# A two-layer hybrid block on one core: a scan step in another order, and Toeplitz tiles loaded in 32 rows and filled on the chip

## The chip, the cores and the metric

The kernel runs on one core of a Trainium2 chip. Its time is the time in microseconds (us) of one execution on the device; three runs of a kernel are given with their median. The profile is one more execution, recorded by the hardware profiler.

Five engines work side by side and wait for each other through semaphores: PE (TensorE, matmuls; its weight loads are listed apart as PEld), DVE (VectorE, elementwise work and reductions), ACT (ScalarE, activation functions and copies), POOL (GpSimd) and SP (SyncE, which only issues DMAs). Each engine takes its instructions strictly in the order of its own queue. An instruction that waits for a semaphore holds up everything behind it on that engine. SP, ACT and POOL can issue DMAs; an issue stands in the engine's queue like any other instruction.

## The reference, cut to what matters

The program is eight sublayers in a row, each added to x (2 x 2048 tokens of 256). Two of them are touched. The first is a selective scan: for each of 256 channels and 16 complex states a serial recurrence over 2048 tokens.

```python
def step(h, inp):
    x_t, dt_t, B_t, C_t, xr_t = inp
    h_carrier = h.mean(axis=1)
    T = jnp.cos((c_phase(xr_t) - c_phase(h_carrier)) / 2.0) ** 2
    alpha = jnp.exp(dt_t[..., None] * A_neg)
    expo = 1.0 + (1.0 - alpha) * KAPPA * (1.0 - T[:, None, :])
    mag, ph = (c_mag(h), c_phase(h))
    cmag = jnp.minimum(jnp.exp(expo * jnp.log(mag + 1e-08)), 10.0)
    h = from_polar(cmag, ph)
    Bx = B_t[:, None, :, :] * (dt_t * x_t)[:, :, None, None]
    h = h + Bx
    h = from_polar(jnp.tanh(c_mag(h)), c_phase(h))
    y_t = jnp.einsum('bnc,bdnc->bd', C_t, h)
    return (h, y_t)
```

The fifth is a long convolution: a projection to 512 channels, a four-tap convolution with SiLU, a convolution over 1024 taps with a filter of its own for each channel (written as an FFT, computed in the kernel as products with Toeplitz matrices), a gate and a projection back.

```python
x_f = jnp.fft.rfft(x, n=n)
k_f = jnp.fft.rfft(k_ssm, n=n)
y = jnp.fft.irfft(x_f * k_f[None], n=n)[..., :Lq]
y = y + x * D_skip[None, :, None]
y = y * _silu(z)
return jnp.einsum('bhl,dh->bld', y, W_out)
```

## The kernel before, in words

**Scan** (method scan, lines 257 to 550). The state is kept as real and imaginary part in tiles of 128 partitions x 64 elements. A hardware loop of four turns holds 32 groups of 16 steps each, all written out, under a manual schedule: every engine gets its instructions in the order in which the source names them. One step (lines 400 to 489) goes round like this:

- PE multiplies the channel sums hs with the constant mean into hc and hd (line 410), then projects the state of the step before to the output (line 494).
- ACT squares hc (line 418) and makes ci (427, 428). Meanwhile DVE works through gl (414), the product with hd (420), ex (424) and ngd (425). ACT makes ea from ex (429) and fac from ngd and ci (439).
- DVE forms the new state p (436 to 444) and its squared magnitudes m2 and r1 (446 to 453). ACT scales the drive of the next step meanwhile (391).
- ACT then runs twelve activations of 128x64 in a row (459 to 473): logarithms and exponentials that give 1/|h| (ir), e = exp(-2|h|), le = log(1+e), ld = log(1-e), sg = 1/(1+e), 1/|h|^2 (rm) and the small corrections k1 and k2c.
- DVE multiplies p by ir and by e-1 (475, 477), makes dl (480), multiplies by sg into the history tile with the sums hs as a second output (482), and ends with th, kc, lg and kd (486 to 489), which the next step's gl and ex read.

Several results live in small PSUM tiles of the pool pa with one buffer for each name: lm, m (used for le again) and lr (used for lb, the logarithm with 1e-8, again).

**Convolution** (method sublayer_c, lines 1073 to 1244). E = 4 blocks of 128 channels. For each block, kernels(e, g) loads Toeplitz tiles: partition p of a tile row holds the reversed filter from element p on, so one filter read at 64 shifted starts gives 64 rows. A group g is eight channels: SP loads partitions 0 to 63 with four of them, ACT partitions 64 to 127 with four others, 1216 elements long. The pool has three tiles. convolve then issues 9 x 2 x 4 x 2 matmuls of 64 rows x 32 columns with 128 moving columns (line 1170); the input xring is kept as two half blocks of 64 tokens by turn, which transposes with 16 matmuls a chunk (1154). After four groups leave copies the sums out of PSUM on ACT (1181) and stores them to DRAM from ACT's queue (1183). In even groups produce makes a chunk of the next block's input (PE line 1128, ACT copy 1134, DVE 1137 and 1139, ACT SiLU 1141, a POOL store) and finish takes up a chunk of the block before (POOL loads 1190 and 1191, PE 1195, ACT SiLU 1197, DVE 1198 and 1199). In odd groups turn and project follow (PE 1206, DVE 1210). In this part only PE's order is the order of the source; the order of the other engines is a scheduler's.

Of the kernel before, what the change touches and what calls it, by code (L numbers as in the profile page):

```python
# [17 lines left out]
AF = mybir.ActivationFunctionType  # L18
ALU = mybir.AluOpType
# [4 lines left out]
P = 128  # L24
B, S, D = 2, 2048, 256
NT = B * S
NI = NT // P
NB = S // P
# [9 lines left out]
SMALL = 1e-10  # L38
MAG_EPS = 1e-8
# [8 lines left out]
L_CONV = 1024  # L48
TOEP = L_CONV + P
KREV = 1280  # L50
# [3 lines left out]
HALF = P // 2  # L54
# [5 lines left out]
def new(pool, shape, name, **kw):  # L60
    return pool.tile(list(shape), F32, name=name, tag=name, **kw)


class Kernel:
# [192 lines left out]
    def scan(self, y, dtd, dxd, tabd):  # L257
# [6 lines left out]
        tc, nc = self.tc, self.nc  # L264
        V, A, G = nc.vector, nc.scalar, nc.gpsimd
        J, TURN = 64, TG * GROUPS
        with ExitStack() as c:
# [132 lines left out]
            def step(k, g, before, act_gap, dve_gap):  # L400
# [4 lines left out]
                hn = hist[g][:, k]  # L405
# [63 lines left out]
                A.activation(sg, le, AF.Exp, scale=-1.0)  # L469
# [3 lines left out]
                A.activation(k2c, lb, AF.Exp, scale=-0.5)  # L473
                for k2 in range(2):
                    V.tensor_tensor(p[:, k2], p[:, k2], ir, ALU.mult)  # L475
                for k2 in range(2):
                    V.scalar_tensor_tensor(p[:, k2], e, -1.0, p[:, k2], ALU.add, ALU.mult)  # L477
                th, kc, dl = (w([J], n) for n in ("th", "kc", "dl"))

                V.scalar_tensor_tensor(dl, p[:, 0], 0.5 * SMALL, rm, ALU.mult, ALU.mult)  # L480
                for k2 in range(2):
                    V.tensor_tensor_reduce(  # L482
                        out=hn[:, k2], in0=p[:, k2], in1=sg, scale=-1.0, scalar=0.0 if k2 else J * SMALL,
# [1 line left out]
                    )  # L485
                V.tensor_tensor(th, ld, le, ALU.subtract)
                V.scalar_tensor_tensor(kc, k2c, 2.0 * MAG_EPS, k1, ALU.mult, ALU.add)
                V.scalar_tensor_tensor(lg[o], th, 2.0, kc, ALU.mult, ALU.add)
                V.scalar_tensor_tensor(kd[o], kc, 0.5, dl, ALU.mult, ALU.add)

# [582 lines left out]
    def sublayer_c(self):  # L1073
# [7 lines left out]
        tc, nc = self.tc, self.nc  # L1081
        V, A, G = nc.vector, nc.scalar, nc.gpsimd
        E, TAPS = 4, L_CONV // P
        W = L_CONV + P + HALF
        with ExitStack() as c:
            dp = c.enter_context(tc.tile_pool(name="c_dram", bufs=1, space=DRAM))
            yd = dp.tile([E * P, NB, B, P], F32, name="c_yd", tag="c_yd")
# [8 lines left out]
            xring = [new(kp, [P, HALF, 2, TAPS + NB, B], f"c_x{j}") for j in range(2)]  # L1096
            for t in xring:
                G.memset(t[:, :, :, 0:TAPS], 0.0)
# [12 lines left out]

            with tc.tile_pool(name="c_ln", bufs=2) as lp, tc.tile_pool(name="c_pl", bufs=2, space=PSUM) as pl:
# [10 lines left out]
            def produce(e, ch):  # L1123

                b, i0, cs = ch // 4, ch % 4 * 4, slice(ch * CH, (ch + 1) * CH)
                ps = new(pp, [P, CH], "ps")
                for k in range(2):
                    nc.tensor.matmul(ps, wi[:, k, e * P : (e + 1) * P], xT[:, k, cs], start=k == 0, stop=k == 1)
                xin = new(xp, [P, 3 + CH], "c_xi")
                if i0 == 0:  # L1130
                    V.memset(xin[:, 0:3], 0.0)
                else:
                    V.tensor_copy(xin[:, 0:3], last[0][:, CH : CH + 3])
                A.copy(xin[:, 3:], ps)
                last[0] = xin
                acc = new(tp, [P, CH], "c_acc")
                V.tensor_scalar(acc, xin[:, 0:CH], cw[:, e, 0:1], cb[:, e : e + 1], ALU.mult, ALU.add)
                for j in range(1, 4):
                    V.scalar_tensor_tensor(acc, xin[:, j : j + CH], cw[:, e, j : j + 1], acc, ALU.mult, ALU.add)
                xs = new(tp, [P, CH], "c_xs")  # L1140
                A.activation(xs, acc, AF.Silu)
                G.dma_start(out=xd[e * P : (e + 1) * P, cs], in_=xs)
                return e, ch, xs

            def turn(e, ch, xs):

                b, i0 = ch // 4, ch % 4 * 4
                ps = new(pt, [P, 2, 4, HALF], "ps_t")
                for h in range(2):
                    for j in range(4):  # L1150
                        for r in range(2):
                            rows = slice(r * HALF, (r + 1) * HALF)
                            lo = j * P + h * HALF
                            nc.tensor.matmul(
                                ps[rows, h, j, :], xs[:, lo : lo + HALF], self.ident[:, rows], start=True, stop=True
                            )
                for h in range(2):
                    V.tensor_copy(
                        xring[e % 2][:, :, h, TAPS + i0 : TAPS + i0 + 4, b], ps[:, h].rearrange("p j c -> p c j")
                    )  # L1160

            def convolve(e, g, t, ps):
                x = xring[e % 2]
                for m in range(TAPS + 1):
                    for h in range(2):
                        lo = L_CONV - m * P + h * HALF
                        for j in range(4):
                            for r in range(2):
                                rows = slice(r * HALF, (r + 1) * HALF)
                                nc.tensor.matmul(  # L1170
                                    ps[r][j * 32 : (j + 1) * 32, g % 4, :],
                                    x[rows, 4 * g + j, h, TAPS - m : TAPS - m + NB, :].rearrange("p i b -> p (i b)"),
                                    t[rows, j, lo : lo + P],
                                    start=m == 0 and h == 0, stop=m == TAPS and h == 1,
                                )

            def leave(e, g, ps):

                for r in range(2):
                    ys = new(tp, [P, 4, P], "c_ys")  # L1180
                    A.copy(ys, ps[r][:, :, ::-1])
                    rows = slice(e * P + r * HALF + 4 * g, e * P + r * HALF + 4 * g + 16)
                    A.dma_start(
                        out=yd[rows].rearrange("(s j) i b t -> (j i b) s t", j=4), in_=ys
                    )

            def finish(e, ch):
                b, i0, cs = ch // 4, ch % 4 * 4, slice(ch * CH, (ch + 1) * CH)
                yc, xs = new(tp, [P, CH], "c_yc"), new(tp, [P, CH], "c_xs")
                G.dma_start(out=yc.rearrange("p (i t) -> p i t", t=P), in_=yd[e * P : (e + 1) * P, i0 : i0 + 4, b])  # L1190
                G.dma_start(out=xs, in_=xd[e * P : (e + 1) * P, cs])
                ps = new(pp, [P, CH], "ps")
                z0 = E * P + e * P
                for k in range(2):
                    nc.tensor.matmul(ps, wi[:, k, z0 : z0 + P], xT[:, k, cs], start=k == 0, stop=k == 1)
                sz = new(tp, [P, CH], "c_acc")
                A.activation(sz, ps, AF.Silu)
# [24 lines left out]
                later(turn, t)  # L1222
            later(turn)
            for e in range(E):
                for g in range(HALF // 4):
                    t = kernels(e, g)
                    if g % 4 == 0:
                        ps = [new(pc, [P, 4, P], f"ps_c{r}") for r in range(2)]
                    convolve(e, g, t, ps)
                    if g % 4 == 3:  # L1230
                        leave(e, g - 3, ps)
                    if g % 2 == 0:
                        work = []
                        if e + 1 < E:
                            work.append((turn, produce(e + 1, g // 2)))
                        if e > 0:
                            work.append((project, finish(e - 1, g // 2)))
# [469 lines left out]
```

## Time and profile before

| | us |
|---|---|
| median of three runs | 14147.37 (14145.97 to 14152.4) |
| profiled execution, its own time | 14151.41 |
| its span, first to last instruction | 14149.7 |
| up to the scan's loop | 335 |
| after the scan, up to the convolution's start (10170 to 11095) | 925 |
| norm and first chunks of the convolution (11095 to 11171) | 76 |
| after the convolution's loop (from 12170) | 1980 |

Over the span DVE is busy 10378.9 us, ACT 8647.8, PE 5571.1 and POOL 415.6. The longest waits inside the scan, from the view of who waited for whom (engine, line, released by: total us, times, longest):

```profile
ACT lm L459 <- DVE m L451: 1216.4, 2047, 1.1
ACT sq L418 <- PE hc L410: 1168.8, 2043, 0.9
DVE p L475 <- ACT ir L463: 1063.2, 2047, 0.6
...
DVE p L436 <- ACT ea L429: 323.1, 2047, 1.6
```

They are the places of a step at which one engine stands until another hands over: each occurs once in each of the 2048 steps. A wait on a line says nothing of what comes behind it in the same queue; for that the timeline is read. In the page and the timeline a tile is named by what the program called it, with numbers left out, so m stands for m, m2 and le, and lr for lr, ln and lb.

### The profile page before, as it was taken

What the parts mean: (1) busy time and instruction counts of PE and PEld (TensorE: products, weight loads), DVE (VectorE), ACT (ScalarE), POOL (GpSimd) and SP (SyncE); (2) the same over time, 40 slices, a digit from 0 to 9 for tenths busy, and PEclk for the clock granted to TensorE, in tenths of its full rate; (3) what the DMA queues carried; (4) which work ended last, traced back from release to release, by engine and by line L of the source; (5) the groups of instructions that cost most, each with busy time, mean ns of one, the idle gap of its engine ahead of it and who ended that gap; (6) DMA issues with size and microseconds to landing.
All of it is one profiled execution on the core that took longest, in us unless ns stands there. A gap on an engine that the chain in (4) does not pass through costs nothing. (4 is left out here: it accounts for less than half of the span.)

```text
span 14149.7 us, 282029 instructions
## 1 busy us (share of the span) xinstructions
PE 5571.1 (39%) x76456; PEld 3830.2 (27%) x76456; DVE 10378.9 (73%) x65267; ACT 8647.8 (61%) x44978; POOL 415.6 (3%) x496
## 2 busy tenths in 40 slices
PE   4222222222222222222222222222389655778888
PEld 2111111111111111111111111111255444544445
DVE  6888888888888888888888888888757411355555
ACT  3777777777777777777777777777535100234444
POOL 0000000000000000000000000000000000031110
PEclk6555555555555555555555555555579787889999
DMA  3000000000000000000000000000000477342220
GB/s 79 14 17 14 17 15 15 17 14 17 16 14 17 14 17 17 14 17 14 17 17 14 17 14 17 17 14 17 10 13 1 105 186 187 86 99 34 34 33 20
DMA packets 349182, 461.08 MB, mean 33 GB/s; under 512 B 205026, under 2 KB 245033, under 8 KB 346548
## 3 DMA queue, kind: packets, MB, share of 16 engines
q1 hardware_dynamic: 296372, 319.91, 10.0%
q10 hardware_dynamic: 36352, 88.61, 2.6%
q0 software_dynamic: 14848, 34.36, 0.9%
q8 instruction: 611, 10.01, 0.3%
q14 instruction: 999, 8.18, 0.2%
HBM read 385.55 MB, written 52.46 MB: 31 GB/s over the span
## 5 line engine op out<-in xcount | busy, mean ns | idle before, releaser
L410 PE MATMUL hc<-hs,mean 128*32 128x2 f32 x16384 | 588.4, 203 | 7238.6 <-DVE hs L482 7174.4
L410 PEld LDWEIGHTS hc<-hs,mean 128*32 128x32 f32 x16384 | 413.0, 140 | 7450.7 <-DVE hs L482 7386.1
L475 DVE TENSOR_TENSOR p<-p,ir 128x64 f32<-128x64 f32 x4096 | 739.6, 222 | 1063.8 <-ACT ir L463 1063.8
L494 PE MATMUL yps<-cs,hist 128*64 128x8 f32 x8192 | 1225.0, 259 | 13.4 <-DVE hs L482 13.4
L459 ACT ACTIVATE lm<-m 128x64 f32<-128x64 f32 x2048 | 466.3, 228 | 1217.1 <-DVE m L451 1217.1
L391 ACT ACTIVATE bx<-dx,tc 128x64 f32<-128x64 f32 x4098 | 1170.7, 333 | 0.1
L418 ACT ACTIVATE sq<-hc 128x2 f32<-128x2 f32 x2048 | 352.6, 172 | 1169.7 <-PE hc L410 1169.7
L1531 ACT ACTIVATE d_p<-ps_e 128x512 f32<-128x512 f32 (+3 forms) x1280 | 599.6, 537 | 755.4 <-PE ps_o L1512 532.0
L494 PEld LDWEIGHTS yps<-cs,hist 128*64 128x64 f32 x8192 | 1033.3, 218 | 45.5 <-DVE hs L482 13.8
L482 DVE CUSTOM_DVE_ANT_0 hist<-p,sg 128x64 f32<-128x64 f32 x4096 | 751.5, 220 | 11.9 <-DVE hs L482 6.0
L442 DVE TENSOR_TENSOR p<-p,fac 128x64 f32<-128x64 f32 x4096 | 741.7, 222 | 8.9 <-DVE p L437 6.5
L477 DVE SCALAR_TENSOR_TENSOR p<-e,p 128x64 f32<-128x64 f32 x4096 | 739.6, 222 | 9.9 <-ACT sg L469 9.2
L444 DVE TENSOR_TENSOR p<-p,bx 128x64 f32<-128x64 f32 x4096 | 726.9, 219 | 2.5
L439 ACT ACTIVATE fac<-ngd,ci 128x64 f32<-128x64 f32 x2048 | 712.7, 348 | 1.0 <-DVE p L436 1.0
L436 DVE SCALAR_TENSOR_TENSOR p<-hist,ea 128x64 f32<-128x64 f32 x2048 | 462.0, 226 | 323.2 <-ACT ea L429 323.2
L1524 PE MATMUL ps_e<-d_qt,d_kt 128*128 128x512 f32 (+3 forms) x1280 | 556.4, 444 | 45.7 <-ACT d_p L1531 36.4
L410 PE MATMUL hd<-hs,mean 128*32 128x2 f32 x16384 | 545.2, 193 | 0.0
L429 ACT ACTIVATE ea<-ex 128x64 f32<-128x64 f32 x2048 | 525.6, 257 | 24.4 <-DVE ex L424 5.2
L1481 PE MATMUL ps_m<-d_kt,d_qt 128*128 128x512 f32 (+3 forms) x1280 | 498.9, 436 | 98.5 <-DVE d_part L1486 38.8
L1170 PE MATMUL ps_c<-toep,c_x 64*32 64x128 f32 x18432 | 383.4, 320 | 385.2 <-issue 384.1
L432 PE MATMUL hd<-ident,ci 128*1 128x1 f32 x4096 | 386.7, 163 | 354.3 <-ACT ci L428 346.8
L1491 DVE TENSOR_REDUCE d_part<-ps_m 128x1 f32<-128x512 f32 x768 | 495.0, 684 | 41.6 <-PE ps_m L1481 40.7
(448 smaller groups left out, 22020.5 us busy)
## 6 DMA issues: line engine op xcount, KB each, us to landing
toep<-in_C_krev ACTq DMA_DIRECT2D x64, 1216.0 KB, 14.0
toep<-in_C_krev SPq DMA_DIRECT2D x64, 1216.0 KB, 9.8
ng<-dtd SPq DMA_DIRECT2D x258, 256.0 KB, 3.7
dx<-dxd SPq DMA_DIRECT2D x258, 256.0 KB, 4.2
d_kt<-d_kd SPq DMA_DIRECT2D x128, 128.0 KB, 4.3
d_qt<-d_qd SPq DMA_DIRECT2D x128, 128.0 KB, 3.9
y<-ys SPq DMA_DIRECT2D x512, 8.0 KB, 1.9
c_xd<-c_xs POOLq DMA_DIRECT2D x32, 256.0 KB, 6.6
```

The costliest lines, as they stand in the source:

```text
L391: A.activation(bx[o][:, k2], tg[j][2][:, k], AF.Identity, scale=tg[j][0][:, k2, k : k + 1], bias=0.0 if k2 else SMALL,)
L410: nc.tensor.matmul(out[r : r + 32], mean[:, r : r + 32], hs[i], start=True, stop=True)
L429: A.activation(ea, ex, AF.Exp)
L439: A.activation(fac, ngd, AF.Exp, scale=ci)
L442: V.tensor_tensor(p[:, k2], p[:, k2], fac, ALU.mult)
L444: V.tensor_tensor(p[:, k2], p[:, k2], bx[o][:, k2], ALU.add)
L475: V.tensor_tensor(p[:, k2], p[:, k2], ir, ALU.mult)
L477: V.scalar_tensor_tensor(p[:, k2], e, -1.0, p[:, k2], ALU.add, ALU.mult)
L482: V.tensor_tensor_reduce(out=hn[:, k2], in0=p[:, k2], in1=sg, scale=-1.0, scalar=0.0 if k2 else J * SMALL, op0=ALU.mult, op1=ALU.add, accu ...
L494: nc.tensor.matmul(yps[:, k, :], hist[g][:, k, k2], tg[g][3][:, k2, k], start=k2 == 0, stop=k2 == 1)
L1524: nc.tensor.matmul(s[:, q0:], ks[kt // 4][:, hh, kt % 4 * P : (kt % 4 + 1) * P], q[:, hh, q0:], start=True, stop=not diag,)
L1531: A.activation(pr[:, q0:], s[:, q0:], AF.Exp, scale=0.25)
```

## The change

In the scan's step the activations behind e stand in another order: the logarithm with 1e-8 (lb, now a PSUM tile of its own) comes right behind e, then le, sg, rm, k2c, ld and k1. dl is computed after the new state instead of before it, from the stored state and rm, and stands behind kc. In the convolution a group is four channels instead of eight, and a tile holds each of them over all 128 partitions. SP loads 32 partitions (0 to 31) of two channels, ACT 32 partitions (96 to 127) of the two others, 1248 elements long; DVE copies the first pair upwards in two steps (32 rows, then 64), ACT the second pair downwards in two steps. The matmuls are 128 rows x 32 columns; there are 9 x 4 in a group, and 128 groups. turn uses four transposes. A chunk of produce and finish now falls in every fourth group.

```diff
                 A.activation(e, m, AF.Exp, scale=-2.0)
-                A.activation(rm, lm, AF.Exp, scale=-1.0)
+                lb, k1, k2c = wa("lb"), w([J], "k1"), w([J], "k2c")
+                A.activation(lb, m2, AF.Ln, bias=MAG_EPS)
                 le = wa("m")
                 A.activation(le, e, AF.Ln, bias=1.0)
+                A.activation(sg, le, AF.Exp, scale=-1.0)
+                A.activation(rm, lm, AF.Exp, scale=-1.0)
+                A.activation(k2c, lb, AF.Exp, scale=-0.5)
                 A.activation(ld, e, AF.Ln, scale=-1.0, bias=1.0)
-                A.activation(sg, le, AF.Exp, scale=-1.0)
-                lb, k1, k2c = wa("lr"), w([J], "k1"), w([J], "k2c")
-                A.activation(lb, m2, AF.Ln, bias=MAG_EPS)
                 A.activation(k1, rm, AF.Ln, scale=MAG_EPS, bias=1.0)
-                A.activation(k2c, lb, AF.Exp, scale=-0.5)
...
-                V.scalar_tensor_tensor(dl, p[:, 0], 0.5 * SMALL, rm, ALU.mult, ALU.mult)
                 for k2 in range(2):
                     V.tensor_tensor_reduce(
                         out=hn[:, k2], in0=p[:, k2], in1=sg, scale=-1.0, scalar=0.0 if k2 else J * SMALL,
...
                 V.tensor_tensor(th, ld, le, ALU.subtract)
                 V.scalar_tensor_tensor(kc, k2c, 2.0 * MAG_EPS, k1, ALU.mult, ALU.add)
+                V.scalar_tensor_tensor(dl, hn[:, 0], -SMALL, rm, ALU.mult, ALU.mult)
                 V.scalar_tensor_tensor(lg[o], th, 2.0, kc, ALU.mult, ALU.add)
...
-        W = L_CONV + P + HALF
+        Q = P // 4
+        W = L_CONV + P + P - Q
...
                 for r in range(2):
-                    first = kr.offset + (e * P + r * HALF + 4 * g) * KREV
+                    first = kr.offset + (e * P + 4 * g + 2 * r) * KREV
                     (nc.scalar if r else nc.sync).dma_start(
-                        out=t[r * HALF : (r + 1) * HALF],
-                        in_=bass.AP(kr.tensor, first, [[1, HALF], [KREV, 4], [1, W]]),
+                        out=t[r * (P - Q) : r * (P - Q) + Q, 2 * r : 2 * r + 2],
+                        in_=bass.AP(kr.tensor, first, [[1, Q], [KREV, 2], [1, W]]),
                     )
+                a, b = t[:, 0:2], t[:, 2:4]
+                V.tensor_copy(a[Q : 2 * Q, :, 0 : W - Q], a[0:Q, :, Q:W])
+                V.tensor_copy(a[2 * Q : P, :, 0 : W - 3 * Q], a[0 : 2 * Q, :, 2 * Q : W - Q])
+                A.copy(b[2 * Q : 3 * Q, :, Q:W], b[3 * Q : P, :, 0 : W - Q])
+                A.copy(b[0 : 2 * Q, :, 3 * Q : W], b[2 * Q : P, :, Q : W - 2 * Q])
                 return t
...
-                for h in range(2):
-                    for j in range(4):
-                        for r in range(2):
-                            rows = slice(r * HALF, (r + 1) * HALF)
-                            lo = j * P + h * HALF
-                            nc.tensor.matmul(
-                                ps[rows, h, j, :], xs[:, lo : lo + HALF], self.ident[:, rows], start=True, stop=True
-                            )
+                for j in range(4):
+                    nc.tensor.transpose(ps[:, j, :], xs[:, j * P : (j + 1) * P], self.ident)
...
                 for m in range(TAPS + 1):
-                    for h in range(2):
-                        lo = L_CONV - m * P + h * HALF
-                        for j in range(4):
-                            for r in range(2):
-                                rows = slice(r * HALF, (r + 1) * HALF)
-                                nc.tensor.matmul(
-                                    ps[r][j * 32 : (j + 1) * 32, g % 4, :],
-                                    x[rows, 4 * g + j, h, TAPS - m : TAPS - m + NB, :].rearrange("p i b -> p (i b)"),
-                                    t[rows, j, lo : lo + P],
-                                    start=m == 0 and h == 0, stop=m == TAPS and h == 1,
-                                )
+                    for j in range(4):
+                        lo = L_CONV - m * P + j // 2 * (P - Q)
+                        nc.tensor.matmul(
+                            ps[j * 32 : (j + 1) * 32, g % 4, :],
+                            x[:, 4 * g + j, TAPS - m : TAPS - m + NB, :].rearrange("p i b -> p (i b)"),
+                            t[:, j, lo : lo + P], start=m == 0, stop=m == TAPS,
+                        )
...
-                for g in range(HALF // 4):
+                for g in range(P // 4):
...
-                    if g % 2 == 0:
+                    if g % 4 == 0:
                         work = []
...
-                    else:
+                    elif g % 4 == 2:
                         for f, args in work:
```

More of the change, by code (lines that the diff above doesn't have):

```diff
@@ L1095, in sublayer_c @@
             dk = self.load_cols(kp, "C_D_skip")
-            xring = [new(kp, [P, HALF, 2, TAPS + NB, B], f"c_x{j}") for j in range(2)]
+            xring = [new(kp, [P, P, TAPS + NB, B], f"c_x{j}") for j in range(2)]
             for t in xring:
-                G.memset(t[:, :, :, 0:TAPS], 0.0)
+                G.memset(t[:, :, 0:TAPS], 0.0)
             kb = c.enter_context(tc.tile_pool(name="c_kb", bufs=3))
@@ L1147, in turn @@
                 b, i0 = ch // 4, ch % 4 * 4
-                ps = new(pt, [P, 2, 4, HALF], "ps_t")
-                for h in range(2):
-                    for j in range(4):
-                        for r in range(2):
-                            rows = slice(r * HALF, (r + 1) * HALF)
-                            lo = j * P + h * HALF
-                            nc.tensor.matmul(
-                                ps[rows, h, j, :], xs[:, lo : lo + HALF], self.ident[:, rows], start=True, stop=True
-                            )
-                for h in range(2):
-                    V.tensor_copy(
-                        xring[e % 2][:, :, h, TAPS + i0 : TAPS + i0 + 4, b], ps[:, h].rearrange("p j c -> p c j")
-                    )
+                ps = new(pt, [P, 4, P], "ps_t")
+                for j in range(4):
+                    nc.tensor.transpose(ps[:, j, :], xs[:, j * P : (j + 1) * P], self.ident)
+                V.tensor_copy(
+                    xring[e % 2][:, :, TAPS + i0 : TAPS + i0 + 4, b], ps.rearrange("p j c -> p c j")
+                )
             def convolve(e, g, t, ps):
@@ L1164, in convolve @@
                 for m in range(TAPS + 1):
-                    for h in range(2):
-                        lo = L_CONV - m * P + h * HALF
-                        for j in range(4):
-                            for r in range(2):
-                                rows = slice(r * HALF, (r + 1) * HALF)
-                                nc.tensor.matmul(
-                                    ps[r][j * 32 : (j + 1) * 32, g % 4, :],
-                                    x[rows, 4 * g + j, h, TAPS - m : TAPS - m + NB, :].rearrange("p i b -> p (i b)"),
-                                    t[rows, j, lo : lo + P],
-                                    start=m == 0 and h == 0, stop=m == TAPS and h == 1,
-                                )
-            def leave(e, g, ps):
[L1179 to L1185, printed above, removed]
+                    for j in range(4):
[4 more added lines that the diff above has]
+                            t[:, j, lo : lo + P], start=m == 0, stop=m == TAPS,
+                        )
+            def leave(e, g, ps):
+                ys = new(tp, [P, 4, P], "c_ys")
+                A.copy(ys, ps[:, :, ::-1])
+                rows = slice(e * P + 4 * g, e * P + 4 * g + 16)
+                A.dma_start(out=yd[rows].rearrange("(s j) i b t -> (j i b) s t", j=4), in_=ys)
             def finish(e, ch):
@@ L1224, in sublayer_c @@
             for e in range(E):
-                for g in range(HALF // 4):
+                for g in range(P // 4):
                     t = kernels(e, g)
                     if g % 4 == 0:
-                        ps = [new(pc, [P, 4, P], f"ps_c{r}") for r in range(2)]
+                        ps = new(pc, [P, 4, P], "ps_c")
                     convolve(e, g, t, ps)
@@ L1231, in sublayer_c @@
                         leave(e, g - 3, ps)
-                    if g % 2 == 0:
+                    if g % 4 == 0:
                         work = []
                         if e + 1 < E:
-                            work.append((turn, produce(e + 1, g // 2)))
+                            work.append((turn, produce(e + 1, g // 4)))
                         if e > 0:
-                            work.append((project, finish(e - 1, g // 2)))
-                    else:
+                            work.append((project, finish(e - 1, g // 4)))
+                    elif g % 4 == 2:
                         for f, args in work:
```

## The prediction

> **What bounds the kernel now.** I read the table of busy time by stretches first, then the timeline of one scan step, then the timeline and waits of the convolution.
>
> ```profile
> 335.00:10170.00 9835.00, 2274.09 (x45030) 1839.52 (x45030) 8314.08 (x59762) 7254.69 (x42110) 0.00 (x0) 0.50 0.06 15
> ...
> 11171.00:12170.00 999.00, 595.72 (x19563) 449.98 (x19569) 151.17 (x262) 59.72 (x102) 45.23 (x74) 0.79 0.75 182
> ```
>
> After bounds and length stand busy us of PE, PEld, DVE, ACT, POOL, then clock, DMA share, GB/s. The scan is 9835 of 14149.7 us: 2048 serial steps of 4.80 us. The convolution loop is 999 us with DVE and ACT almost idle. The change touches both.
>
> One step, from the timeline (start, duration, engine, line):
>
> ```profile
> 5002.30 0.36 DVE L477 SCALAR_TENSOR_TENSOR p<-e,p 128x64 f32<-128x64 f32 x2
> 5002.39 0.20 ACT L469 ACTIVATE sg<-m 128x64 f32<-128x64 f32 x1
> ...
> 5002.63 0.23 DVE L480 SCALAR_TENSOR_TENSOR dl<-p,rm 128x64 f32<-128x64 f32 x1
> ...
> 5002.78 0.22 DVE L482 CUSTOM_DVE_ANT_0 hist<-p,sg 128x64 f32<-128x64 f32 x1
> 5002.79 0.21 ACT L473 ACTIVATE k2c<-lr 128x64 f32<-128x64 f32 x1
> ...
> 5003.20 0.22 DVE L487 SCALAR_TENSOR_TENSOR kc<-k2c,k 128x64 f32<-128x64 f32 x1
> ...
> 5003.45 0.22 DVE L488 SCALAR_TENSOR_TENSOR lg<-th,kc 128x64 f32<-128x64 f32 x1
> ...
> 5003.73 0.22 DVE L414 TENSOR_TENSOR gl<-lg,ng 128x64 f32<-128x64 f32 x1
> ...
> 5003.98 0.23 DVE L424 TENSOR_TENSOR ex<-kd,gl 128x64 f32<-128x64 f32 x1
> ...
> 5004.06 0.17 ACT L428 ACTIVATE ci<-lr 128x1 f32<-128x1 f32 x1
> ...
> 5004.24 0.26 ACT L429 ACTIVATE ea<-ex 128x64 f32<-128x64 f32 x1
> ```
>
> See that ea starts 0.03 after ex ends (5003.98+0.23): DVE's tail, not the PE and ACT branch through ci, releases the next step. DVE issues independent operations 0.14 apart; a value made by the instruction just before costs 0.25 (kc to lg), so there is an empty slot of 0.11 between them.
>
> The convolution: PE in one group of eight channels, 288 records.
>
> ```profile
> 11604.48 1.54 PE L1170 MATMUL ps_c<-toep,c_x 64*32 64x128 f32 x90
> ...
> 11608.99 3.26 PE L1170 MATMUL ps_c<-toep,c_x 64*32 64x128 f32 x128 [2.96 <-issue]
> ...
> 11617.39 2.35 PE L1170 MATMUL ps_c<-toep,c_x 64*32 64x128 f32 x70 [5.15 <-issue]
> ```
>
> ```profile
> toep<-in_C_krev ACTq DMA_DIRECT2D x64, 1216.0 KB, 14.0
> toep<-in_C_krev SPq DMA_DIRECT2D x64, 1216.0 KB, 9.8
> ng<-dtd SPq DMA_DIRECT2D x258, 256.0 KB, 3.7
> ```
>
> PE works 7.15 us and stands 8.1 us inside the group without a semaphore, while DMA is 75% busy. The breaks come at 128 records, so I take them for instruction fetch behind a full DMA; that is an inference. PE with its feed is the bound, at 999/32 = 31.2 us for sixteen channels.
>
> **What the Trainium skill says.** "VectorE: DVE Perf Modes", Mode 2×_2P: a single-source fp32 operation between SBUF tiles makes two elements a cycle. The trace agrees: TENSOR_SCALAR 128x2048 takes 1.22 us (L300), 0.52 ns an element. "ScalarE: Activation LUTs", What ACT_TABLE_LOAD costs: 186 ns + 0.833 ns per element with immediates, neighbours overlapping by 93 ns. The trace agrees: L387 takes 400 ns for 256 and 1042 for 1024. "TensorEngine Tiling (Array Packing)", Available Configurations: 64×32 has eight tiles, 128×32 four. So half as many matmuls, each of twice the depth, need the same array time. The trace fits: the records of L1512 in the form 128*32 128x128 last 279 ns in the mean, those of L1170 269 (median), so one does not grow.
>
> **Scan, step by step.** Clock zero is the start of e (L464). Before: le 0.25, ld 0.41, sg 0.55, k2c 0.95 (ends 1.16); DVE L477 0.46, dl 0.79, hist 0.94, th 1.22, kc 1.36, lg 1.61, gl 1.89, ex 2.14, ea 2.40.
> - ACT after: lb 0.11, le 0.25 (it waits for e in both orders), sg 0.51 (le lasts 0.228, plus 0.03), rm 0.62, k2c 0.73, ld 0.84, k1 0.98, which ends 1.23 (0.243 long). The same twelve operations; sg gains only 0.04, and ld and the last one come later.
> - DVE: dl leaves its slot at 0.79, hist takes it (sg ends 0.72, and hist now carries dl's double wait). So hist is 0.15 earlier and with it the branch PE, sq, ci.
> - The tail does not follow fully. th has to wait for ld (0.84+0.24+0.03 = 1.11, its slot being 1.07), kc for k1 (1.26 instead of 1.36). dl at 1.40 fills the empty slot: lg 1.54, kd 1.67, gl 1.81, ex 2.06.
> - ex is 0.08 earlier; ea, fac and the next step follow it, as ci has 0.15 in hand. No PE, DMA or drive work changes. I take 0.075 x 2048 = -154 us. Bounds: 0.03 (sg's wait or k1 comes 0.04 later than worked out) to 0.13 (ACT spacing hides both waits): -61 to -266.
>
> **Convolution.** Groups are now four channels: 128 of them, each with two loads of 32x2x1248x4 B = 312 KB (before 64 groups, two of 1216 KB). Bytes of toep fall from 155.6 to 79.9 MB (KB taken as 1000). Conv matmuls fall from 9216 to 4608. Added per group on DVE: copies of 2432 and 2304 elements, 1.42 and 1.36 us (0.52 ns an element + 0.15). On ACT 2432 and 2304 elements: by L387's slope 2.21 and 2.11, minus overlap 2.12 and 2.02. DVE has room: four groups add 11.1 us to about 6.5 of own work in 29. ACT becomes the bound, and its queue is in order. In a round of four groups (A the last of one set, B, C, D of the next) it stands in the instruction order as: load A, load B, first copies A and B, second copies A and B, load C, c_ys, load D, c_yd issue, c_xi, first copy C, c_acc, second copy C, first copy D, c_xs, second copy D. Each load is issued shortly before ACT needs it.
> - Busy: eight copies 16.6; four issues 2.5 (0.63 each); c_ys, c_xi, c_acc, c_xs 2.0 and c_yd 0.5. Sum 21.6 us.
> - Wait 1, load A landing. A line between 256 KB in 3.7 and 1216 KB in 9.8 to 14.0 gives 4.1 to 4.3 for 312 KB; I take 4.5. ACT has issued both at 1.3: 3.3 us.
> - Wait 2, c_ys for conv A. Conv of a group is 72 records: 34 ns each at twice the rate of the first burst shown (2.5 us), 51 at the second (3.7); I take 3.0, with 2.4 and 4.3 as ends. Conv A runs from 10.9 (second copy of A) to 13.9: 0.5 us.
> - Wait 3, c_xi for conv B and the four L1128 records (2.8): 13.9+3.0+2.8 = 19.7 against 15.6: 4.2 us.
> - Round 29.6 us. The eight rounds of the last block have no c_xi and c_xs: 26.3. Sum 24 x 29.6 + 8 x 26.3 = 921; stage change -78 us.
> The fetch breaks I cost at nothing now: PE waits for copies most of a round, and needs half the instructions. If they stayed as long as before, with two on the PE legs of a round, conv would be near the 4.3 end (997, no gain). turn's sixteen small matmuls become four transposes, on PE away from ACT's chain: nothing. POOL's issues do not change. The loads queued on SP wait only for a free buffer and land while ACT copies.
>
> Sum: 14149.7 - 154 - 78 = 13918 of span; 1.7 us lie around the span, and the median of the runs is 4.0 below the profiled run: 13915.
>
> **Rivals.**
> 1. Slower: load landing on ACT. If a 312 KB load lands in 10 us (1216 KB took 9.8 and 14.0; only 32 rows take it now), waits for A and then also for C lie bare: rounds 40.6 and 37.3, stage about 1270, +272. Total 14151-154+272 -> 14265. It decides from about 8 us (rounds near 36, stage 1143). Against it: 256 KB took 3.7 and total traffic halves. Chance 0.09.
> 2. The scan follows hist fully (0.15 x 2048 = -307; ACT's last four are spaced closer than 0.11): with -78 it gives 13762. Against: ld alone is 0.24 long. Chance 0.10.
> 3. The scan gains nothing visible (-20) because k1 and ld come late, stage as forecast: 14050. Chance 0.10.
> 4. The convolution eats its part: copies on DVE at one element a cycle (2.7 and 2.55 us) or fetch breaks as before; stage 1000 to 1040, total 13993 to 14035, 14015 in the middle. For: the pieces are 32 or 64 partitions in two runs, of which no row shows the rate. Chance 0.21.
> 5. Forecast: 0.50.
>
> **Numbers.** 13915; range 13780 to 14060, which leaves rival 1, part of rival 2 and tails out. A measurement here can tell 0.2% (28 us) from no change. Faster: rivals 2 to 5 almost whole, 0.88; same 0.03 (rival 3 or 4 with a landing of 6 to 7 us); slower 0.09.
>
> **What would show it.** Scan: step period 4.67 instead of 4.75 (kc came next at 5007.95); hist 0.33 after L477; th and kc released by ACT; dl between kc and lg without idle. If ex moves by 0.15 or by nothing, the late ld and k1 were mis-sized. Convolution: ACT near 70% busy, loads landing in 4 to 5 us, a round of about 30 us, waits of ACT on toep loads and on L1128. If landing is over 8 us, or DVE's copies take 2.5 us, my stage sum is wrong.

## The result: time and profile after

The changed kernel takes 13921.02 us (median of four runs, 13913.98 to 13927.47). The kernel before took 14148.51 us beside it (four runs, 14145.97 to 14152.4). The ratio is 0.9839, with a 95% interval of 0.9822 to 0.9856. The forecast of 13915 us and its sign hold; the two terms of its sum were both off by about 35 us, in opposite directions, so that the total fits this closely is luck. The profiled execution took 13913.98 us, its span is 13912.3.

First the table of busy time by stretches, in the columns explained above: the scan's loop, then the convolution's loop.

```profile
335.00:10051.00 9716.00, 2274.80 (x45052) 1840.12 (x45052) 8248.48 (x59781) 7367.66 (x42122) 0.00 (x0) 0.50 0.06 16
...
11051.80:11938.20 886.40, 558.69 (x9692) 424.39 (x9696) 497.80 (x489) 595.83 (x353) 62.78 (x74) 0.78 0.45 123
```

| stage, us | before | after | difference | forecast |
|---|---|---|---|---|
| scan's loop | 9835 | 9716 | -119 | -154 |
| up to the convolution, its norm and first chunks | 1001 | 1000.8 | 0 | 0 |
| convolution's loop | 999 | 886.4 | -113 | -78 |
| after it | 1980 | 1974 | -6 | 0 |

The stages are those of the two profiled executions, whose spans differ by 237 us; the medians differ by 228.

In the convolution ACT has gone from 60 to 596 us of work and DVE from 150 to 498, PE has kept its 560 to 600, and the DMA engines are busy for 0.45 of the stretch instead of 0.75.

One scan step after the change, from the timeline (start, duration, engine, line):

```profile
5000.25 0.22 ACT L464 ACTIVATE e<-m 128x64 f32<-128x64 f32 x1
...
5000.76 0.22 ACT L469 ACTIVATE sg<-m 128x64 f32<-128x64 f32 x1
...
5001.09 0.23 DVE L480 CUSTOM_DVE_ANT_0 hist<-p,sg 128x64 f32<-128x64 f32 x1
5001.09 0.27 ACT L472 ACTIVATE ld<-e 128x64 f32<-128x64 f32 x1
5001.24 0.27 ACT L473 ACTIVATE k<-rm 128x64 f32<-128x64 f32 x1
...
5001.39 0.22 DVE L484 TENSOR_TENSOR th<-ld,m 128x64 f32<-128x64 f32 x1
5001.53 0.23 DVE L485 SCALAR_TENSOR_TENSOR kc<-k2c,k 128x64 f32<-128x64 f32 x1
5001.68 0.22 DVE L486 SCALAR_TENSOR_TENSOR dl<-hist,rm 128x64 f32<-128x64 f32 x1
5001.81 0.22 DVE L487 SCALAR_TENSOR_TENSOR lg<-th,kc 128x64 f32<-128x64 f32 x1
```

Set e's start to zero. dl has moved into the empty slot between kc and lg, as forecast. th starts 0.03 after ld ends (5001.09 + 0.27) and kc 0.03 after k1 ends (5001.24 + 0.27): ACT's last two results release the tail. hist starts at 0.84 where 0.79 was forecast, although sg had ended at 0.73. In the median over all steps of the two traces a step is 4.692 us long instead of 4.753; kc starts at 1.284 instead of 1.361, ex at 2.085 instead of 2.142.

The convolution, part of one round of four groups (DMA issues stand under ACTq; k in "xk" counts records):

```profile
11505.51 3.84 PE L1165 MATMUL ps_c<-toep,c_x 128*32 128x128 f32 x72 [3.61 <-ACT toep L1114]
...
11509.12 0.63 ACT L1146 ACTIVATE c_xs<-c_acc 128x512 f32<-128x512 f32 x1 [1.43 <-DVE c_acc L1144]
11509.13 0.80 ACTq L1106 DMA_DIRECT2D toep<-in_C_krev  x2
...
11509.78 2.11 ACT L1114 COPY toep<-toep 64x2304 f32<-64x2304 f32 x1
...
11512.73 2.21 ACT L1113 COPY toep<-toep 32x2432 f32<-32x2432 f32 x1 [0.84 <-DMA toep<-in_C_krev]
...
11523.89 1.98 PE L1133 MATMUL ps<-c_xT,w_C_W_inT 128*128 128x512 f32 x4
```

and what ACT's loads of a tile took (count, KB each, median us from issue to landing; SP's took the same), and the waits of the loop (total us, times, longest):

```profile
toep<-in_C_krev ACTq DMA_DIRECT2D x128, 312.0 KB, 4.7
```

```profile
PEld ps_c L1165 <- ACT toep L1114: 330.7, 83, 7.2
...
ACT c_xi L1139 <- PE ps L1133: 75.1, 20, 7.7
...
ACT toep L1113 <- DMA toep<-in_C_krev: 53.8, 38, 5.0
...
PEld ps_c L1165 <- issue: 33.9, 64, 0.8
```

PE now stands for ACT's second copy. Its breaks without a semaphore are nearly gone: 33.9 us in the loop, against 444.9 for the same entry of before. A group's 72 matmul records run in one piece (3.84 us). The two load issues at 11509.13 run while ACT is at work on c_xs: the engine goes on with its work while its queue issues. Over the whole loop the 125 load issues of ACT that fall in it take 46.0 us, and 41.7 of them lie under other work of ACT.

### The profile page after: what moved, and what is told of

It is laid out like the page before. It is cut to its first block, busy times and chain, and to the rows that moved or that the text cites. A ratio compares the mean times of both kernels' runs of the same rounds, so it can differ in the third digit from the quotient of the medians.

```text
span 13912.3 us, 263001 instructions
## 1 busy us (share of the span) xinstructions
PE 5521.0 (40%) x66344; PEld 3798.1 (27%) x66344; DVE 10663.1 (77%) x65491; ACT 9306.1 (67%) x45234; POOL 432.4 (3%) x496
## 5 line engine op out<-in xcount | busy, mean ns | idle before, releaser
L472 ACT ACTIVATE ld<-e 128x64 f32<-128x64 f32 x2048 | 548.2, 268 | 0.0
L473 ACT ACTIVATE k<-rm 128x64 f32<-128x64 f32 x2048 | 544.1, 266 | 0.0
L1165 PE MATMUL ps_c<-toep,c_x 128*32 128x128 f32 x9216 | 407.5, 341 | 306.6 <-ACT toep L1114 304.9
```

## The experiments

### Each half alone

scan_only has the scan's lines of after in the kernel before, conv_only the convolution's.

> The scan step of after with the convolution of before. Forecast's mechanism, with the size that the trace of after shows: the scan's loop takes 0.058 us less a step, so 119 us less, 14030 in all (14020 to 14040), and the convolution loop stays at 999. Rival: the order of the scan has nothing to do with the 119 us (the granted clock, or tiles placed elsewhere in memory by the smaller Toeplitz tiles): then this kernel is within 20 us of before, about 14148.

> The convolution of after with the scan step of before. Parts that simply add: loop of the convolution 886 us instead of 999, so 113 us less, 14035 in all (14025 to 14045), and the scan stays at 4.80 us a step. Rival: the parts are not independent, and this kernel gains 78 us or less (14070) or more than 150 (13995).

Measured, against 14150.31 of before: scan_only 14024.88 us (ratio 0.9912, 0.9895 to 0.9928), conv_only 14044.07 (0.9926, 0.9910 to 0.9943). That is -125 and -106, in sum -231; the whole change gave -228. The halves add, and each stage of the trace is the work of its own edit: the convolution's loop takes 994 us in scan_only and 887 in conv_only.

### The two edits of the scan, each alone

dl_only leaves ACT's order as before and moves only dl:

```diff
-                V.scalar_tensor_tensor(dl, p[:, 0], 0.5 * SMALL, rm, ALU.mult, ALU.mult)
...
                 V.scalar_tensor_tensor(kc, k2c, 2.0 * MAG_EPS, k1, ALU.mult, ALU.add)
+                V.scalar_tensor_tensor(dl, hn[:, 0], -SMALL, rm, ALU.mult, ALU.mult)
```

> Before, with the one edit that dl is computed from the stored state and stands behind kc; ACT's order is that of before. The prediction's arithmetic: hist takes dl's slot, 0.79 us after e, lr and k1 are early enough in the old order (k1 ends 1.05), kc comes at about 1.21, and the step gains 0.12 us or more: -250 us, 13900. Account formed on the trace of after: hist starts 0.11 after sg has ended since it now waits for two engines at once; in the old order sg ends at 0.75, so hist starts at 0.86 and kc at 1.28, a gain of 0.05 a step: -90 to -115 us, 14035 to 14060; ACT's new order would then be worth no more than 20 us. Third: dl's move gains nothing by itself (14148), and all of the 119 us are ACT's order.

Measured: 13976.78 us (0.9880, 0.9863 to 0.9896), -174. None of the three accounts hit it. The timeline:

```profile
5001.74 0.22 ACT L464 ACTIVATE e<-m 128x64 f32<-128x64 f32 x1
...
5002.58 0.23 DVE L480 CUSTOM_DVE_ANT_0 hist<-p,sg 128x64 f32<-128x64 f32 x1
...
5003.01 0.22 DVE L485 SCALAR_TENSOR_TENSOR kc<-k2c,k 128x64 f32<-128x64 f32 x1
...
5003.28 0.22 DVE L487 SCALAR_TENSOR_TENSOR lg<-th,kc 128x64 f32<-128x64 f32 x1
```

Here the six DVE instructions from hist (two halves) to lg stand 0.13 to 0.15 apart without a gap: kc at 1.27 and lg at 1.54 after e. The step is 4.667 us, shorter than in after. So one edit of the two does all of the gain in the scan, and more: ACT's new order costs 48 us beside it (14024.88 less 13976.78, both measured against the same runs).

act_only does the reverse, with dl in its old place and ACT's new order:

> Before, with ACT's new order alone; dl stands in its old place ahead of hist. If dl's wait decides: rm now comes behind sg (0.63 us after e instead of 0.11), dl can start at about 0.95 instead of 0.79, hist follows at 1.09 instead of 0.94, and the step is 0.13 to 0.15 us longer: +265 to +305 us, 14415 to 14455. If ACT's order is a gain by itself (sg 0.04 earlier, nothing else on the path): -80 us, 14070. If the order of ACT makes no difference: 14148.

Measured: 14312.85 us (1.0117, 1.0101 to 1.0134), +163. The direction is that of dl's wait, the size is not; from the timeline:

```profile
5003.19 0.22 ACT L470 ACTIVATE rm<-lm 128x64 f32<-128x64 f32 x1
...
5003.44 0.23 DVE L479 SCALAR_TENSOR_TENSOR dl<-p,rm 128x64 f32<-128x64 f32 x1
```

dl starts 0.03 after rm has ended, not 0.11; the step is 0.08 longer. So ACT's new order is a loss both ways: 163 us without dl's move, 48 beside it.

### The wait of hist

After lost 0.04 at hist and 0.02 at kc against the forecast. dl_tiny (on dl_only) and after_tiny (on after) give DVE's part of hist's wait to a copy of one column:

```diff
+                V.tensor_copy(w([1], "pw"), p[:, 0, 0:1])
                 for k2 in range(2):
                     V.tensor_tensor_reduce(
```

> dl_only with one copy of a single column of p (128x1) on DVE between L477 and hist: the small copy waits for DVE's own p, and hist then waits for ACT's sg alone. Theory A (hist starts 0.83 us after e, 0.07 after sg's end, because it has to wait for two engines at once): with one wait it starts about 0.03 after sg's end, like other DVE instructions behind ACT, that is at 0.79 to 0.81; kc follows, 0.02 to 0.04 a step: 13895 to 13940 against dl_only's 13977. Theory B (this instruction can't start nearer to the second half of L477, which ends at 0.83, whatever it waits for): hist stays at 0.83 or later by the small copy: 13975 to 14060.

Measured: dl_tiny 13881.64 us (0.9813, 0.9796 to 0.9829), 95 below dl_only (90 when each is taken against the before beside it), more than either bound. hist starts at 0.807 instead of 0.833 (median over the steps), its second half follows after 0.140 instead of 0.151, and th starts at 1.093 instead of 1.130. An added instruction makes the step shorter, by 0.043. So waiting for two engines at once costs this instruction about 0.03 of its start, and its second half comes sooner too.

The traces show how. Ahead of an instruction with two waits DVE has a semaphore instruction of its own, 0.021 long, that takes one of them. In before, after and dl_only it starts 0.728 to 0.730 after e (medians). In before the next instruction, dl, starts 0.066 behind it; in after and dl_only the next one is hist, and it starts 0.105 behind it. In dl_tiny and after_tiny hist has no such instruction ahead of it. In act_only dl has it too, but rm ends only at 0.848, and dl starts 0.033 after that: the price shows where the last signal comes early.

> After with the small copy of dl_tiny, so that hist waits for sg alone. In the trace of after kc stands behind two limits that lie 0.01 us apart: hist, its second half and th give it a slot at 1.274 us after e, k1's end at 1.252 lets it start at 1.284. If that reading is right, an earlier hist moves neither th (it waits for ld, 1.140) nor kc: hist starts at 0.78 to 0.81, kc stays at 1.28, gain 0 to 20 us: 13900 to 13921. If the wait of hist for two engines is what cost after its missing 35 us: kc follows hist, 70 to 95 us: 13825 to 13850.

Measured: after_tiny 13898.06 us (0.9829, 0.9813 to 0.9846), 14 us below after by the ratios, a difference that lies within their intervals. The timeline:

```profile
5004.48 0.27 ACT L472 ACTIVATE ld<-e 128x64 f32<-128x64 f32 x1
...
5004.62 0.27 ACT L473 ACTIVATE k<-rm 128x64 f32<-128x64 f32 x1
...
5004.77 0.22 DVE L485 TENSOR_TENSOR th<-ld,m 128x64 f32<-128x64 f32 x1
...
5004.92 0.23 DVE L486 SCALAR_TENSOR_TENSOR kc<-k2c,k 128x64 f32<-128x64 f32 x1
```

hist comes earlier (0.807 in the median), but th still starts at ld's end plus 0.03 (5004.48 + 0.27) and kc at k1's end plus 0.03; the median step is 4.692 us as in after. The same remedy that gives 95 us in ACT's old order gives at most a small part of it in the new one. With hist early, ld (by way of th and one slot more) and k1 both put kc at 1.284. What a shorter ld and k1 would bring isn't shown by a run; by the reading above the late hist would still hold kc at 1.274.

### A slot that is free in after

th_gap has the convolution of after, the scan of dl_only, and th moved ahead of hist:

```diff
+                V.tensor_tensor(th, ld, le, ALU.subtract)
                 for k2 in range(2):
                     V.tensor_tensor_reduce(
...
-                V.tensor_tensor(th, ld, le, ALU.subtract)
```

> After, with ACT's order of before in the scan (ld, k1 and k2c early again), dl behind kc as in after, and th moved ahead of hist, into the slot between the end of L477 and hist (0.74 to 0.83 us after e) that is empty in the trace of after. Without th's move the parts add to about 13870 (dl_only 13977 less conv_only's 106). Theory (hist, then two slots, then kc is the path; ld is ready at 0.65): hist starts 0.04 later, kc 0.07 to 0.09 earlier, a gain of 0.05 to 0.07 a step: 13730 to 13770. Rival 1: hist's branch over PE, sq and ci takes over at once (hist 0.04 later): 13870 to 13950. Rival 2: hist starts a full slot later behind th (0.14), nothing is gained: 13850 to 13890.

Measured: 13752.23 us (0.9730, 0.9714 to 0.9747), as the theory has it in time. Its steps differ: in the median th starts at 0.794, sg's end plus 0.03, though it doesn't read sg, and hist a slot later at 0.933 (rival 2's step); but kc follows hist's second half directly at 1.221 against 1.264 of dl_only, and the step is 4.621 us. So th came only halfway into the slot and put hist 0.10 later, not the 0.04 of the theory; the time came out by another way. th now carries the wait for ACT; hist has no wait for ACT and no semaphore instruction ahead of it. Behind sg the same four instructions follow each other as in dl_tiny, where th stands in its old place: there kc starts at 1.227 and the step is 4.624. What both runs take away is hist's double wait; that th's place adds anything to it is not shown.

### What PE's breaks came from

quarter takes the kernel before and loads a tile in every fourth group:

```diff
-                    t = kernels(e, g)
                     if g % 4 == 0:
+                        t = kernels(e, g)
```

> Before, with Toeplitz tiles loaded only in every fourth group and used by four groups: three quarters of the loads, and the right filters for three quarters of the channels, are left out; matmuls, copies and stores are as before. Prediction's inference (the breaks of PE inside a group are instruction fetch that stands behind the Toeplitz transfers): the breaks shrink from 8.1 us a group to 1 or 2, the convolution loop falls from 999 us to between 560 and 750, in all 13710 to 13900. Rival: fetch of 18000 matmul instructions takes its time whatever else the DMA engines do: breaks stay, loop above 930, in all over 14080.

Measured: 13862.97 us (0.9806, 0.9790 to 0.9822) against 14133.13. Its loop:

```profile
11163.50:11884.50 721.00, 508.84 (x19577) 379.95 (x19578) 151.17 (x263) 59.79 (x103) 45.20 (x74) 0.91 0.33 86
```

With the same number of matmuls and without three quarters of the loads the loop loses 278 us, and the breaks 205 of 444.9: 239.9 us are left of that entry in its view of waits. The transfers did lengthen the breaks. But 3.7 us a group stay (239.9 / 64; in before 444.9 / 64 = 7.0, the group shown having 8.1), more than the 1 or 2 of the inference, and their number stays too (147 for 143): the breaks have a part of their own.

That they are instruction fetch can be read from the trace of before. It has a DMA queue for instructions (queue, kind: packets, MB, share of 16 engines; in the loop):

```profile
q8 instruction: 152, 2.49, 1.1%
```

Each packet has 16 KB, and there is one for every 256 of PE's records (matmuls and weight loads: 39132 in the loop of before for 152 packets, 19388 in that of after for 76). Of the 88 breaks of more than 1 us, 77 end 1.2 to 1.7 us after such a packet has ended, where 8% of points chosen at random do. In before the packet begins 2.8 us after PE has stopped; in quarter it begins 0.7 us before (medians). There 84 of 88 breaks end so, and they last 1.8 us instead of 5.6 (medians). So beside the loads the packets come late, and what stays without most of the loads is the fetch itself.

PE's work fell by 87 us as well, at a granted clock of 0.91 instead of 0.79; why the clock rose wasn't tried.

### What bounds the convolution after

sp_loads issues both loads of a tile from SP; rows64 loads ACT's two channels in 64 rows, so that ACT has one copy left:

```diff
-                    (nc.scalar if r else nc.sync).dma_start(
+                    nc.sync.dma_start(
```

```diff
-                        out=t[r * (P - Q) : r * (P - Q) + Q, 2 * r : 2 * r + 2],
-                        in_=bass.AP(kr.tensor, first, [[1, Q], [KREV, 2], [1, W]]),
+                        out=t[HALF:P, 2:4, 0 : W - Q] if r else t[0:Q, 0:2],
+                        in_=bass.AP(kr.tensor, first, [[1, HALF if r else Q], [KREV, 2], [1, W - Q if r else W]]),
...
-                A.copy(b[2 * Q : 3 * Q, :, Q:W], b[3 * Q : P, :, 0 : W - Q])
-                A.copy(b[0 : 2 * Q, :, 3 * Q : W], b[2 * Q : P, :, Q : W - 2 * Q])
+                A.copy(b[0:HALF, :, HALF : W - Q], b[HALF:P, :, 0 : W - Q - HALF])
...
-                        lo = L_CONV - m * P + j // 2 * (P - Q)
+                        lo = L_CONV - m * P + j // 2 * HALF
```

> After, with both Toeplitz loads issued from SP, none from ACT. Account of the trace of after (ACT's queue is the bound of the loop, and its own issues, 128 x 0.33 us, and its waits for loads, 54 us, lie on it): loop 886 us -> 790 to 830, in all 13820 to 13865. Rival: ACT then waits as long for something else (DMA landing on one queue, PE, DVE), loop 870 to 890, in all 13905 to 13925. Slower (over 13930) if two loads on one queue land later than 6 us.

> After, with ACT's two channels loaded in 64 rows (1216 long, 622 KB) instead of 32, so that ACT makes one copy of 2304 elements a group instead of two; DVE's side is as in after. ACT's queue the bound: 128 x 2.21 us of copies fall away, less some 1 to 1.5 us of later landing where it lies bare: loop 886 us -> 640 to 740, in all 13675 to 13775. Rival, PE with its feed the bound again: loop over 850, in all over 13885. Rival, landing: 622 KB land in 8 us or more, half the gain is lost: loop 760 to 820, in all 13795 to 13855.

Measured: sp_loads 13888.42 us (0.9826, 0.9809 to 0.9842), its loop 866 us, 21 less than after: the rival, that other waits step in. rows64 13825.54 (0.9784, 0.9767 to 0.9800), its loop 801 us, 85 less, in the range of the rival on landing, though the load (622 KB of 1000 bytes, 608 of the profile's) lands in 6.6 us and not in 8 or more. The waits say where the rest went; those of rows64:

```profile
ACT toep L1113 <- DMA toep<-in_C_krev: 168.4, 65, 6.5
DVE toep L1111 <- DMA toep<-in_C_krev: 138.7, 53, 7.1
```

In sp_loads ACT's 54 us of waits for loads go, but c_ys waits 123.5 us for ps_c (34.3 in after). The edit does more than move loads: the scheduler gives ACT and DVE another order. In after ACT makes the copies of one more group before each c_ys (9, 13, 17 groups are copied ahead of the second to fourth); in sp_loads c_ys stands directly behind the last copy of its own four groups (8, 12, 16) and waits for that group's matmuls. And the 42 us of issues (128 x 0.33) were never on ACT's path: all but 4 lay under its other work. So sp_loads does not tell what the queue of a load is worth by itself. In rows64 ACT works only 318 us, but both copying engines stand for the loads. So "ACT's queue is the bound" is true of its order (c_ys and c_xi stand behind PE, the copies behind them), and not of its work alone.

### A faster version

best joins the scan of th_gap, the copies of rows64 and both loads on SP; best2 leaves each load on its queue of after.

> The scan of th_gap with the convolution of rows64 and both loads on SP. Parts add: scan -161 against after (th_gap against after on the step: 4.634 for 4.719 us), 64 rows -86. Loads on SP are issued as soon as a buffer is free, so of ACT's 168 us of waits for loads in rows64 a third to a half goes: -50 to -80 more. In all 13595 to 13640, against 13921 of after. Rival: the landing (6.6 us) is bound by the three buffers, not by ACT's queue, and SP gains nothing: 13660 to 13690.

> The scan of th_gap with the convolution of rows64, each load on its queue of after. If the loss of best against the sum of its parts came from both loads in one queue (its loop takes 834 us, that of rows64 801): the loop is at 800 again, the scan at 4.63 us a step, 13655 to 13680. Rival: the loop depends on what ran before it, or the parts do not add: 13690 to 13720, as best.

Measured: best 13696.98 us (0.9683, 0.9667 to 0.9699); its loop takes 834 us, more than rows64's 801, though the loads alone gained 21 in sp_loads. That is in neither range of the expectation. In its view of waits PEld stands 180.7 us for DVE's second copy (12.7 in rows64): DVE's copies have become PE's last wait. Their loads aren't the reason. DVE's copies wait 1.9 us for them (138.7 in rows64) and ACT's 3.4 (168.4), and the small loads land in 4.1 us (5.5), the large ones in 6.7 (6.6). What DVE stands for is

```profile
DVE c_acc L1141 <- ACT c_xi L1138: 134.9, 24, 8.0
```

against 21.5 us in rows64. As in sp_loads, the order has changed with the edit: in best the four c_acc of a chunk stand nearly in a row, with copies behind them, in rows64 and best2 they stand between the copies.

best2 takes the loads apart again, and has the order of rows64 again: 13660.93 us (0.9663, 0.9647 to 0.9679), the loop at 806, in the range of its theory. It can't tell the shared queue from the order; the waits speak for the order, and no run has both loads on SP in the order of rows64. It is faster than both kernels of the case: 479 us below before (14139.89), where the change as it stands gave 228.

## Why the prediction was right, and which terms of it were off

**Scan, -154 forecast, -119 measured.** The mechanism was right: dl in the empty slot, hist earlier, the tail following only in part because ld and k1 release th and kc; ea still follows ex. The size was off in the step "kc for k1 (1.26)": it took k1 to end at 1.23 with the length it had in the kernel before, 0.243. In the new order ld lasts 0.268 (0.240 before) and k1 0.266, k1 ends at 1.252, kc starts at 1.284, and all that follows is 0.025 late: 0.058 a step instead of 0.075. The other late step is hist, at 0.834 for 0.79: the forecast let hist carry dl's double wait at dl's price, but hist starts 0.105 after the semaphore instruction and dl 0.066. after_tiny shows that hist isn't the cause alone: with hist at 0.807 kc stays where it was. Nor are ld and k1 quite alone: had they been as short as forecast, the late hist would have left kc at about 1.274 (an estimate from the spacing in after's trace, not run). The two mis-sized terms lie 0.01 apart.

The forecast also counted ACT's order as part of the gain, by sg's 0.04. sg did come earlier (0.511 for 0.558), but hist made nothing of it: in dl_only, with the later sg, it starts at 0.833 as well. dl's move alone takes 174 us, the order gives 48 back. The forecast had the price in its own list, "ld and the last one come later", and didn't weigh it against a sum without the order.

**Convolution, -78 forecast, -113 measured.** DVE's copies (1.42 and 1.36 forecast, 1.42 and 1.35 measured), the landing (4.5 and 4.7) and ACT's queue, more by its order than by its work, as what sets the round were right. A round took 27.7 us (886.4 / 32) where the forecast's mean is 28.8 (921 / 32). Its terms for ACT:

| term, us a round | forecast | measured |
|---|---|---|
| eight copies | 16.6 | 17.1 (4 x 2.21 + 4 x 2.11, less an overlap of 0.2) |
| four load issues | 2.5 | 0.1 (4.2 / 32; they take 4 x 0.33, nearly all under other work) |
| c_ys, c_xi, c_acc, c_xs | 2.0 | 2.4 (0.59, 0.59, 0.60, 0.63) |
| wait for loads | 3.3 | 1.7 (53.8 / 32) |
| wait of c_ys | 0.5 | 1.1 (34.3 / 32) |
| wait of c_xi | 4.2 | 3.1 (75.1 / 24) |
| wait of c_xs for DVE | none | 2.5 (59.6 of the view of waits / 24) |

The largest error lies in the load issues and what follows from them. The forecast let ACT begin them when its other work was done, as an issue that stands in the engine's queue suggests, and so had the landing bare. In the trace loads A and B are issued during c_xs, 0.65 us before second copy D begins. This stretch and the copy (2.11) cover more than half of the landing, and the wait for loads is half of the forecast's. Copies overlap only where neighbours belong to different groups, by 0.09, and not the second copy with the first that it reads. L1133 (L1128 of before) takes 1.98 us and not 2.8. The wait of c_xs for DVE's chain was left out, and the wait of c_acc for PE in the last eight rounds (28.7 us) isn't named; conv itself takes 3.84 and not 3.0. The breaks, costed at nothing, cost next to nothing (33.9 us), as forecast, and their cause, called an inference there, holds (quarter and its queue of instructions).

One reading is loose: L300's 1.23 us are 0.60 ns for each of 2048 elements; 0.52 is what is left when the fixed 0.15 us of the copies' sum is taken off first.

**The rivals.** Landing of 8 us or more (rival 1): 4.7. Scan following hist fully (2): no, ld and k1 hold it. Scan gaining nothing (3): its mechanism is the one that took 35 us, not all. DVE's copies at half the rate or breaks that stay (4): neither.

What stays open: why an activation of the same form lasts 0.27 in the new order and 0.24 in the old one. act_only shows the same 0.268 and 0.266 with DVE's work elsewhere in the step, so dl's place isn't it.

## What to carry to other kernels

When a change moves two things on two engines, work out each alone: here one half held all of the gain and the other a loss, and the sum hid it. On an engine that issues in order, filling a slot in which the next instruction would wait anyway is the cheap gain; before crediting an earlier result, look which other input of the same tail has become the last. Work taken from a bound engine is worth only as much as the order of its queue lets through: moving away ACT's load issues and 54 us of its waits gave 21, and removing 278 us of copies gave 85. And where a scheduler orders the engines, an edit of one line can change the order of others: compare the orders before a difference is put down to the line.

## What the runs showed of the hardware

- A DVE instruction that waits for two engines starts later than one that waits for one, even when both have long signalled: hist at 0.833 and 0.834 with sg ended at 0.761 and 0.735, and at 0.807 in both orders when another instruction had taken one of the waits. Behind the semaphore instruction that takes the second wait dl starts after 0.066, hist after 0.105.
- A wait can cover more than an instruction reads: th, moved ahead of hist, started 0.03 after sg, which it doesn't use, and 0.14 after ld had ended; hist behind it then had no wait for ACT.
- ACT's issue of a DMA went with its rows and hardly with its channels: 32 rows x 2 took 0.33 us, 64 x 2 0.60, 64 x 4 0.63. In the loop of after 41.7 of 46.0 us of such issues ran under other work of ACT.
- PE's instructions come by DMA in packets of 16 KB, and beside heavy loads they come late: with DMA 75% busy PE stood 5.6 us at a break (median of those over 1 us), with a quarter of the loads and DMA 33% busy 1.8.
- Two loads of 312 and 608 KB a group on one queue landed in 4.1 and 6.7 us (best), on two queues in 5.7 and 6.4 (best2).
